# A message-passing layer on one core: messages turned by a scaled W_o1, and a longer prepared start

## The chip, the cores and the metric

The kernel runs on one core of a Trainium2 chip. A core has a matrix engine (TensorE, PE in the profile, its weight loads PEld), VectorE (DVE), ScalarE (ACT), GpSimd (POOL) and SyncE (SP), which only issues DMAs. The engines work beside each other, each through its own instructions in order, and wait for one another by semaphores. The metric is the device time of one execution in microseconds, the median of several runs.

## The reference, cut to what matters

There are 12500 nodes with 128 features and 400000 edges, sorted by `dst`. Each edge carries 20 attributes and a weight.

```python
h   = maximum(layernorm(x), 0) @ W_in2f.T
Wij = smu(edge_attr @ W_f1.T + b_f1) @ W_f2.T + b_f2
Wij = Wij * edge_weight[:, None]
agg = segment_sum(h[dst] * Wij, src, num_segments=12500)
out = x + smu(agg @ W_o1.T + b_o1) @ W_o2.T + b_o2
# smu(z) = ((1 + a) z + (1 - a) z erf(mu (1 - a) z)) / 2,  a = 0.01, mu = 2.5
```

Edges read h at `dst`, which is sorted, and are summed at `src`, which is random. smu is built as a factor times (LIN z + gelu(ZS z)); the factor (GC) is folded into the next weights.

## The kernel before, in words

The edges are cut into 3125 tiles of 128, four tiles make a group (782 groups, the last with one tile), two groups make a superblock, which shares its loads. The 98 blocks of 128 nodes are called bins.

**A group's way.** PE makes the hidden layer of the edge network from the attributes (`hide`, L551, tile pu), ScalarE its gelu (`bend`, L559, ge), VectorE adds the linear part (`smooth`, L567, sm), PE multiplies by W_f2 (`weigh`, L604, pw). For h, VectorE compares each edge's `dst`, relative to a window of rows, with a column of numbers (`pick`, L460, the one-hot tile oh), PE multiplies the window of h by it (`gather`, L585, ph; L583 for the first tiles), ScalarE copies the product (`take`, L593, hg). VectorE multiplies both (`mix`, L614, mt). These messages have the features on the partitions; PE transposes them, a tile at a time (`turn`, L624, pt), and ScalarE writes them, times the edge weight, into a message tile (`send`, L634, ms, six buffers). A message's row has 129 numbers: 128 features and its place in its bin, which VectorE copies from `lo_b` (L631).

**Sorting by src.** VectorE and PE count per bin which slot each edge gets (`bins` L485, `count` L499 to L502, `read` L529, `number` L538, tile ix). GpSimd then writes each tile of 128 messages with one indirect DMA to its slots in a buffer in DRAM (L637, buf). This is 3125 scatters, one queue, in order.

**Pieces.** The superblocks are split into nine pieces (59, 59, 59, 59, 48, 37, 27, 27, 16), each with a slot buffer of its own. While piece k is produced, the slots of piece k-1 are read back (`fetch`, L668, tile rw, four ahead, on SP) and summed: VectorE compares the places with a row of numbers (`choose`, L679, se), PE adds up the messages of a bin in PSUM (`add`, L692, pg), and VectorE adds four bins at a time to `agg` in SBUF (L705). A piece's sums can start only after the last scatter of that piece has landed. Then the next piece goes on; in each group some of these sums (`parts`) stand between its own products. The last piece's sums come after the last scatter, in what is called the tail here. There, for each unit of four bins, PE multiplies agg by W_o1 (`half`, L250), ScalarE makes the gelu (L251), VectorE adds the linear part (`bent`, L255), PE multiplies by W_o2 (L260), VectorE adds x and bias (L264), and SP stores. x is loaded by ScalarE's queue four units ahead and given its bias by GpSimd (`with_bias`, L246).

**The start.** The first 24 tiles (`FEW`, three superblocks) are prepared alone: their `dst` and `src` columns are loaded first, and all of them read h of bin 0. The whole columns come in chunks of 512 tiles (`head_of`): fetched, base of each window read off (`based`, L317), spread over the partitions by PE (`spread`, L326), subtracted, transposed and written to DRAM as rows (`written`), from which each superblock loads its own (`targets`). `binned` and `placed` take bin and place from `src` with a shift and a mask on integers (L360 to L365; L721 to L724 for the first tiles). The rows of h for bins 1 to 3 are made in the `opening`, those of the other 94 bins step by step during piece 0: statistics (L190, L191), normalisation (`normed`, L201), transpose (L207), relu (L210), product (L215), and three bf16 parts of the result.

**Order.** The order on PE, VectorE, ScalarE and SP is the order of the program (`manual_schedule`); GpSimd's is set by a scheduler. In the main loop, `step` is called three times in a group. During the opening a call does two of its 14 steps; afterwards a call does about one of the listed `steps`.

## Time and profile before

| what | value |
|---|---|
| median of 3 runs | 4151.15 us (4150.53 to 4153.11) |
| the profiled execution | 4134.27 us, its span 4132.4 us |
| PE busy | 3500.0 us, 85% |
| DVE busy | 3498.8 us, 85% |
| POOL busy | 3048.9 us, 74% |
| ACT busy | 1854.6 us, 45% |
| granted PE clock, mean | 0.959 |
| DMA | 820.60 MB, mean 199 GB/s |

The profile lists groups of instructions by line, with the number of them, the busy time and the mean of one, and names what ended the idle time before them. A timeline line has the start, the duration, the engine, the line of the kernel, the operation, the tiles (written, then read), the shape or the number of instructions merged, and in brackets the idle time of that engine before it and what ended it. A window line has start and end of the window, its length, the busy time and number of instructions of each engine shown, the granted clock, the busy share of the 16 DMA engines and the GB/s moved.

### The profile page before, as it was taken

To read this page: it belongs to the slowest core of one execution; us is meant where nothing else is said; L and a number is where in the kernel's file an instruction comes from. 1 tells how busy PE (TensorE), PEld (TensorE's weight loads), DVE (VectorE), ACT (ScalarE), POOL (GpSimd) and SP (SyncE) were. 2 spreads that over 40 slices of the span, in tenths; PEclk is the share of its full clock that TensorE was granted. 3 is DMA by queue.
4 is the path that set the end of the run, shared out by engine and by line. 5 is a ranking of instruction groups with operands and counts; after the bars stand their busy time and mean duration, and the time that the engine had idled before them with its cause. 6 is when DMAs were issued, how large, how long until landed. Compare 5 with 4: busy or idle time off the path is not lost. (4 is left out here: it accounts for less than half of the span.)

```text
span 4132.4 us, 67973 instructions
## 1 busy us (share of the span) xinstructions
PE 3500.0 (85%) x18032; PEld 2218.3 (54%) x18032; DVE 3498.8 (85%) x8551; ACT 1854.6 (45%) x4810; POOL 3048.9 (74%) x3173
## 2 busy tenths in 40 slices
PE   6767886988887888869888879998799889898888
PEld 2334444555554555545555546665466556565567
DVE  6898886988887988869888869998799889898887
ACT  3446553544444444435444434444344444444431
POOL 4777777777777777777777777777777777777772
PEclk8999998999998999989999989999899999999999
DMA  4875665766656766647666647776588689787568
GB/s 144 234 198 174 189 186 176 211 193 193 196 156 200 211 197 190 199 140 214 214 189 194 201 149 209 215 212 199 173 233 230 176 244 248 211 234 219 170 184 240
DMA packets 564967, 820.60 MB, mean 199 GB/s; under 512 B 178779, under 2 KB 379234, under 8 KB 564444
## 3 DMA queue, kind: packets, MB, share of 16 engines
q1 hardware_dynamic: 450650, 602.06, 51.1%
q0 software_dynamic: 100320, 207.40, 15.2%
q10 hardware_dynamic: 13602, 6.73, 0.6%
q8 instruction: 143, 2.34, 0.3%
q14 instruction: 252, 2.06, 0.2%
HBM read 442.51 MB, written 373.37 MB: 197 GB/s over the span
## 5 line engine op out<-in xcount | busy, mean ns | idle before, releaser
L637 POOL DMA_INDIRECT buf<-ms,ix x3125 | 3008.6, 963 | 1006.6 <-issue 424.8
L634 ACT ACTIVATE ms<-pt,w_sb 128x128 f32<-128x128 f32 x3125 | 890.9, 368 | 1442.2 <-PE pt L624 848.6
L692 PEld LDWEIGHTS pg<-se,rw 128*128 128x128 f32 x8036 | 1060.6, 193 | 267.0 <-issue 225.1
L692 PE MATMUL pg<-se,rw 128*128 128x128 f32 x8036 | 1154.2, 281 | 8.5 <-DVE se L679 8.5
L485 DVE SCALAR_TENSOR_TENSOR so<-irow_ps,hi_f,so 128x98 f16<-128x98 f32 x3116 | 989.8, 318 | 82.6
L624 PE MATMUL pt<-ident,mt 128*128 128x128 f32 x3125 | 507.2, 286 | 524.7 <-DVE mt L614 522.0
L604 PE MATMUL pw<-sm,w_f 128*128 128x512 f32 x1564 | 902.9, 660 | 42.6 <-DVE sm L567 40.7
L551 PE MATMUL pu<-f,w_f 128*128 128x512 f32 x1564 | 824.5, 610 | 0.0
L559 ACT ACTIVATE ge<-pu 128x512 f32<-128x512 f32 x782 | 469.1, 600 | 555.4 <-PE pu L551 540.2
L679 DVE TENSOR_TENSOR se<-irow_ps,rw 128x1536 f32<-128x1536 f32 (+1 forms) x345 | 587.8, 1704 | 148.4 <-DMA rw<-buf 147.2
L614 DVE SCALAR_TENSOR_TENSOR mt<-pw,b,hg 128x512 f32<-128x512 f32 x782 | 583.3, 746 | 145.8 <-ACT hg L593 133.9
L624 PEld LDWEIGHTS pt<-ident,mt 128*128 128x128 f32 x3125 | 348.2, 143 | 624.5 <-DVE mt L614 618.2
L567 DVE SCALAR_TENSOR_TENSOR sm<-pu,ge 128x512 f32<-128x512 f32 x782 | 534.9, 684 | 151.6 <-ACT ge L559 147.1
L593 ACT ACTIVATE hg<-ph 128x512 f32<-128x512 f32 x782 | 469.1, 600 | 170.0 <-PE ph L585 99.6
L529 DVE TENSOR_REDUCE sl<-pc 128x4 f32<-128x392 f32 x782 | 434.7, 556 | 0.0
L604 PEld LDWEIGHTS pw<-sm,w_f 128*128 128x128 f32 x1564 | 240.3, 194 | 164.2 <-DVE sm L567 136.4
L585 PE MATMUL ph<-oh,hw 126*128 126x512 bf16 x776 | 306.4, 395 | 0.0
L551 PEld LDWEIGHTS pu<-f,w_f 128*128 128x128 f32 x1564 | 258.7, 199 | 59.5 <-issue 52.0
L499 PE MATMUL pc<-so,tri 128*128 128x392 f16 x782 | 260.6, 333 | 1.9 <-DVE so L485 1.1
L501 PE MATMUL pc<-so,rest_h 128*128 128x294 f16 x781 | 227.4, 291 | 0.0
L501 PEld LDWEIGHTS <-rest_h 128*128 128x128 f16 x781 | 77.1, 99 | 272.4 <-issue 272.3
L460 DVE TENSOR_SCALAR oh<-rbc,prow 128x1024 bf16<-128x1024 bf16 x388 | 192.8, 497 | 1.5 <-DMA rbc<-rel_dram 1.5
(151 smaller groups left out, 1357.5 us busy)
## 6 DMA issues: line engine op xcount, KB each, us to landing
rw<-buf SPq DMA_DIRECT2D x292, 774.0 KB
rbc<-rel_dram SPq DMA_DIRECT2D x389, 256.0 KB
buf<-zero SPq DMA_DIRECT2D x243, 387.0 KB
buf<-ms,ix POOLq DMA_INDIRECT x3125
buf<-zero SPq DMA_DIRECT2D x193, 258.0 KB
rw<-buf SPq DMA_DIRECT2D x49, 645.0 KB
f<-in_f_t SPq DMA_DIRECT2D x390, 80.0 KB
hw<-h_dram SPq DMA_DIRECT2D x776, 31.5 KB
```

The lines of the kernel that those rows point to most:

```text
L485: nc.vector.scalar_tensor_tensor(so[:, j], irow_ps[:, :NB], hi_f[:, t + j:t + j + 1], so[:, j - 1] if j else before, op0=ALU.is_equal, op1 ...
L551: nc.tensor.matmul(pu[:, :n], w_f1, loaded[g // PER][0][:, o:o + n], start=True, stop=True)
L559: nc.scalar.activation(ge[:, :n], units_of[g][:, :n], AF.Gelu, scale=ZS)
L567: nc.vector.scalar_tensor_tensor(sm[:, :n], units_of.pop(g)[:, :n], LIN, hidden[g][:, :n], op0=ALU.mult, op1=ALU.add)
L593: nc.scalar.activation(hg[:, :n], rows_of[g][:, :n], AF.Copy)
L604: nc.tensor.matmul(pw[:, :n], w_f2, hidden.pop(g)[:, :n], start=True, stop=True)
L614: nc.vector.scalar_tensor_tensor(mt[:, :n], pws.pop(g)[:, :n], b2, rows_of.pop(g)[:, :n], op0=ALU.add, op1=ALU.mult)
L624: nc.tensor.transpose(pt[:, j, :], mt[:, j * P:(j + 1) * P], ident)
L634: nc.scalar.activation(ms[:, j, 0:P], pt[:, j], AF.Copy, scale=w_sb[:, t + j:t + j + 1])
L637: i = nc.gpsimd.indirect_dma_start(out=bufs[k][:, :], out_offset=bass.IndirectOffsetOnAxis(ap=ix[:, j:j + 1], axis=0), in_=ms[:, j, :], in ...
L679: nc.vector.tensor_tensor(se[:, :m], irow_ps.unsqueeze(1).to_broadcast([P, m, P]), rows_in[c][:, :m, P:P + 1].to_broadcast([P, m, P]), op= ...
L692: nc.tensor.matmul(pgs[0][:, g, :], rows_in[c][:, o, 0:P], sel[c][:, o, :], start=(q == 0), stop=(q == Q[k] - 1))
```

## The change

The transpose of a message tile becomes a product with W_o1, which VectorE scales by LIN once at the start. What is scattered and summed is then already LIN (W_o1 message), so the tail no longer multiplies by W_o1: ScalarE takes the gelu straight from agg, and GpSimd adds the linear part. The tail's second product rotates through four PSUM banks instead of two.

The first 48 tiles (six superblocks) are prepared alone instead of 24, a call of `step` does one opening step instead of two, and each further chunk's columns are fetched one chunk before they are used. W_o1 is loaded at the start by ScalarE's queue.

Bin and place come from fp32 arithmetic: `src` is converted, times 1/128 less almost a half, rounded to a whole number by adding and subtracting 12582912, and the place is `src` less 128 times the bin. The normalisation moves from VectorE to ScalarE (scale and bias per partition; `down` is minus mean over deviation). The place column of a message tile is written by ScalarE instead of VectorE.

```diff
-    nc.vector.tensor_scalar(xn[:, j], x_sb[:, b + j, :], mv[:, b + j, 0:1], rstd[:, b + j:b + j + 1],
-                            op0=ALU.subtract, op1=ALU.mult)
+    nc.scalar.activation(xn[:, j], x_sb[:, b + j, :], AF.Identity, scale=rstd[:, b + j:b + j + 1],
+                         bias=down[:, b + j:b + j + 1])
...
-        FEW = 3 * SUP
+        FEW = 6 * SUP
...
+        def whole_bins(to, sf, si):
+            nc.vector.tensor_copy(sf, si)
+            nc.vector.tensor_scalar(to, sf, 1.0 / P, -(P - 1) / (2.0 * P), op0=ALU.mult, op1=ALU.add)
+            nc.vector.tensor_scalar(to, to, ROUND, None, op0=ALU.add)
+            nc.vector.tensor_scalar(to, to, -ROUND, None, op0=ALU.add)
...
             def binned():
-                nc.vector.tensor_scalar(di[:, z:], si[:, z:], 7, None, op0=ALU.arith_shift_right)
-                nc.vector.tensor_copy(hi_f[:, a + z:a + n], di[:, z:])
+                whole_bins(hi_f[:, a + z:a + n], sf[:, z:], si[:, z:])
             def placed():
-                nc.vector.tensor_scalar(di[:, z:], si[:, z:], P - 1, None, op0=ALU.bitwise_and)
-                nc.vector.tensor_copy(lo_b[:, a + z:a + n], di[:, z:])
+                nc.vector.scalar_tensor_tensor(lo_b[:, a + z:a + n], hi_f[:, a + z:a + n], -float(P), sf[:, z:],
+                                               op0=ALU.mult, op1=ALU.add)
...
+        nc.scalar.dma_start(w_o1, w_o1_t)
         nc.scalar.dma_start(x_sb[:, 1:HEAD, :], bin_rows(x, 1, HEAD - 1))
...
+        nc.vector.tensor_scalar(w_o1, w_o1, LIN, None, op0=ALU.mult)
...
-                nc.tensor.transpose(pt[:, j, :], mt[:, j * P:(j + 1) * P], ident)
+                nc.tensor.matmul(pt[:, j, :], mt[:, j * P:(j + 1) * P], w_o1, start=True, stop=True)
...
-            nc.vector.tensor_copy(ms[:, :n, P], lo_b[:, t:t + n])
+            nc.scalar.activation(ms[:, :n, P], lo_b[:, t:t + n], AF.Copy)
...
+        steps.append(heads_of[0].pop(0))
         for c in range(1, NC):
             if loads:
                 steps.append(loads.pop(0))
-            for f in mine:
+            if c + 1 < NC:
+                steps.append(heads_of[c].pop(0))
+            for f in heads_of[c - 1]:
...
             if opening:
-                for _ in range(2):
-                    if opening:
-                        opening.pop(0)()
+                opening.pop(0)()
                 return
...
         def first_half():
             unit = ready.pop(0)
-            po = ps1.tile([P, GRP * P], F32, name=other(0, ("pu", "ph")))
             ge = edge.tile([P, GRP * P], F32, name="ge")
-            half(unit, po, ge)
-            opened.append((unit, po, ge))
+            nc.scalar.activation(ge[:, :width(unit)], part_of(unit), AF.Gelu, scale=ZS / LIN, bias=bz)
+            opened.append((unit, ge))
         def between():
-            unit, po, ge = opened.pop(0)
+            unit, ge = opened.pop(0)
             sm = edge.tile([P, GRP * P], F32, name="sm")
-            bent(unit, po, ge, sm)
+            nc.gpsimd.tensor_add(sm[:, :width(unit)], part_of(unit), ge[:, :width(unit)])
             smoothed.append((unit, sm))
         def second_half():
             unit, sm = smoothed.pop(0)
-            py = ps1.tile([P, GRP, P], F32, name=other(1, ("pw", "pt")))
+            py = ps1.tile([P, GRP, P], F32, name=other(0, ("pu", "ph", "pw", "pt")))
             rest(unit, sm, py)
```

More of the change, by code (lines that the diff above doesn't have):

```diff
@@ L36 @@
 ZP = 128
+ROUND = 12582912.0
 @with_exitstack
@@ L186, in gnn_kernel @@
     rstd = const.tile([P, NB], F32, name="rstd")
+    down = const.tile([P, NB], F32, name="down")
     def stats(pool, b):
@@ L374, in gnn_kernel @@
         dsf = edge.tile([P, FEW], F32, name="dsf", bufs=1)
+        ssf = edge.tile([P, FEW], F32, name="ssf", bufs=1)
         h_first = const.tile([P, 1, 3, D], BF, name="h_first")
@@ L840, in gnn_kernel @@
         steps = [one["placed"], loads.pop(0), one["limits"]]
+        heads_of = [named(lambda c=c: head_of(c),
+                          ("fetched", "based", "spread", "lowered", "turned", "written", "binned", "placed", "limits"))
+                    for c in range(1, NC)]
+        steps.append(heads_of[0].pop(0))
         for c in range(1, NC):
-            mine = named(lambda c=c: head_of(c),
-                         ("fetched", "based", "spread", "lowered", "turned", "written", "binned", "placed", "limits"))
             if loads:
                 steps.append(loads.pop(0))
-            for f in mine:
+            if c + 1 < NC:
+                steps.append(heads_of[c].pop(0))
+            for f in heads_of[c - 1]:
                 steps.append(f)
@@ L879, in gnn_kernel @@
             i = g - g0
-            if g == 2:
-                assert len(opening) == 2
-                targets(3)
+            if g == (FEW // SUP - 3) * PER:
+                assert not opening
             if g % PER == 0:
@@ L952, in other, with part_of @@
             turns[i] += 1
-            return names[turns[i] % 2]
+            return names[turns[i] % len(names)]
+        def part_of(unit):
+            return agg[:, unit[0] * P:unit[0] * P + width(unit)]
         def first_half():
             unit = ready.pop(0)
-            po = ps1.tile([P, GRP * P], F32, name=other(0, ("pu", "ph")))
             ge = edge.tile([P, GRP * P], F32, name="ge")
-            half(unit, po, ge)
-            opened.append((unit, po, ge))
+            nc.scalar.activation(ge[:, :width(unit)], part_of(unit), AF.Gelu, scale=ZS / LIN, bias=bz)
+            opened.append((unit, ge))
         def between():
-            unit, po, ge = opened.pop(0)
+            unit, ge = opened.pop(0)
             sm = edge.tile([P, GRP * P], F32, name="sm")
-            bent(unit, po, ge, sm)
+            nc.gpsimd.tensor_add(sm[:, :width(unit)], part_of(unit), ge[:, :width(unit)])
             smoothed.append((unit, sm))
```

15 lines of the change are left out of this document (7 added, 8 removed).

## The prediction

> **What bounds the kernel now.** I read the scatter line first (source view of L637), then the timeline of GpSimd, then the scatters counted in windows of 100 us; the chain of waits comes last, since it hands the time from engine to engine and gives POOL 0%.
>
> ```profile
> L637 POOL DMA_INDIRECT buf<-ms,ix x3125: 952/958/1427, 19.1 to 4023.8; - x196
> ...
> 2003.26 0.96 POOL L637 DMA_INDIRECT buf<-ms,ix  x1 [0.30 <-issue]
> 2004.52 0.96 POOL L637 DMA_INDIRECT buf<-ms,ix  x1 [0.30 <-DMA buf<-ms,ix]
> ```
>
> One scatter follows the other every 1.263 us (0.96 busy, 0.30 between, whatever is named as releaser). 3125 x 1.263 = 3947 us, and the first and last start lie 4004.7 us apart. GpSimd's queue is the bound; a group of four scatters is 5.05 us.
>
> ```profile
> 0.00:100.00 100.00, 38.76 (x40) 0.83 0.49 143
> 100.00:200.00 100.00, 74.72 (x78) 0.92 0.82 237
> 200.00:300.00 100.00, 75.92 (x80) 0.93 0.71 197
> ...
> 2000.00:2100.00 100.00, 75.91 (x80) 1.00 0.66 204
> ...
> 3900.00:4000.00 100.00, 69.67 (x73) 1.00 0.71 209
> ```
>
> The full rate is 79 to 80 per window. It is missed at the opening (40), a little to 600 us, and at the end (73). So only four things can move the time: the opening, a producer (PE, VectorE, ScalarE) that falls behind 5.05 us per group, the last piece, and the 108.6 us after the last scatter.
>
> ```profile
> 35.32 0.75 DVE L614 SCALAR_TENSOR_TENSOR mt<-pw,b,hg 128x512 f32<-128x512 f32 x1 [4.96 <-ACT hg L593]
> ...
> 59.20 0.26 DVE L317 COPY base_i<-rw 1x128 int32<-1x128 int32 x1 [7.57 <-DMA rw<-in_dst_col]
> 59.76 2.07 PE L326 MATMUL pg<-base_f,ones 1*128 1x512 f32 x2 [8.15 <-DVE base_f L318]
> ...
> 89.83 0.26 DVE L317 COPY base_i<-rw 1x128 int32<-1x128 int32 x1 [4.46 <-DMA rw<-in_dst_col]
> ```
>
> In the opening VectorE waits for the chunk's columns, with everything queued behind it, and PE then runs at half pace (2.07 us for what took 1.12 at 23.59).
>
> ```profile
> 2006.14 0.90 PE L692 MATMUL pg<-se,rw 128*128 128x128 f32 x6
> 2006.88 0.60 PE L624 MATMUL pt<-ident,mt 128*128 128x128 f32 x4
> 2007.38 1.13 PE L604 MATMUL pw<-sm,w_f 128*128 128x512 f32 x2
> ...
> 4054.51 1.02 PE L250 MATMUL ph<-agg,w_o 128*128 128x512 f32 x2
> 4055.37 1.95 PE L692 MATMUL pg<-se,rw 128*128 128x128 f32 x16
> 4057.19 1.13 PE L260 MATMUL pt<-w_o,sm 128*128 128x128 f32 x8
> 4058.15 1.02 PE L250 MATMUL pu<-agg,w_o 128*128 128x512 f32 x2
> 4059.01 1.95 PE L692 MATMUL pg<-se,rw 128*128 128x128 f32 x16
> ```
>
> A transpose is one PE instruction, a 128x128 f32 product two (x8 for four tiles in L260), each about 0.11 us after the one before (sixteen from 4055.37 to 4057.19). The turn rises from four to eight: +0.44 us of PE per group. In the tail PE is full, 3.64 us per unit.
>
> ```profile
> 4070.00:4080.00 10.00, 10.00 (x77) 8.94 (x76) 8.88 (x11) 2.06 (x3) 4.40 (x4) 1.00 1.02 306
> 4110.00:4120.00 10.00, 10.00 (x76) 8.89 (x75) 6.38 (x10) 2.06 (x3) 3.17 (x3) 1.00 0.53 149
> ```
>
> But until about 4100 us the DMA engines are full there too (share 0.9 to 1.02).
>
> **Opening and first piece.** The first scatter of group 11 starts at 106.85, 87.7 us after the first of all; eleven groups at full rate are 55.6: 32.1 us lost. Of this 7.6 and 4.5 are the two column waits; the fetch one chunk ahead removes them (three steps, or about a group, before use for the first chunk, some twenty for the rest). SP gains no transfer; this one moves ahead of a 12-bin load of x. The rest is latency: six opening steps in a group, and a scatter that waits for the place column, which VectorE writes up to 4 us after the turn (26.23 and 30.13 for group 1). ScalarE now writes it just before the weighting. One opening step per call instead of two, over 48 tiles, leaves per group, on VectorE, about 3.5 us by starts (counting 1.3, mt 0.7, sm 0.6, reading 0.5, small ones 0.4) and one or two steps. Walked through with these rows, turns start near 18, 25, 30, 35, 40, 46 us and then every 5 us, against 17.8, 26.2, 36.1, 42.1, 49.2, 64.3. Costs: eight instead of four turns (+0.44), one more operation on the 48 columns (0.15; the 4.85 us stall of L721 stays, since GpSimd still fills its buffers there), the first normalisation on ScalarE (0.2): the first scatter is 0.8 later. Bounds: -12 (column waits alone) to -32 (all). The walk leaves about 10: **-22**.
> Up to the next piece's first scatter at 655.57 another 8.3 us are lost (548.7 against 107 x 5.05). VectorE, 85 to 90% busy there, sheds 28 us (L201 to ScalarE), 5 us of later column waits and the 0.07 to 0.12 us that each cast holds it; the fp32 binning gives back about 0.7 x 6 = 4 (five operations, 0.43 + 3 x 0.45 + 0.68, for four, 1.79). Bounds 0 to -8: **-5**. ScalarE's additions have no row of their own: the place copy lies between 0.20 (128x1) and 0.37 (128x128), I take 0.2, the nearer in size, in the 0.91 us that ScalarE waits for the turn; a normalisation 0.37 like L634, on an engine 58% busy. The wait for a free ms tile (L631, 37.7 us in 35) moves with the copy to ScalarE, which has the same wait in its own rows (474.5); hg and ge queue behind it, but it lasts only while scatters are waiting. W_o1 now leaves on ScalarE's queue ahead of x for bins 1 to 3, one issue of 0.4 us; those bins are issued at 1.66 and read at 10.78.
>
> **Pieces 1 to 8.** Where the producer isn't held back its groups take 3.04 + 0.111 n when PE is full, n being the L692 instructions in them (4.15 at 10, 4.38 at 12, 4.60 at 14, 4.83 at 16, by starts of L624), and up to 5.8 when se and agg keep VectorE busy and PE waits 0.3 to 1.7 us before the turn. Means, by starts: pieces 1 to 3 4.67 (664.2 to 879.2, 46 groups), then 4.83, 4.81, 5.07, 4.91 and 5.47. Only groups that PE fills, about half, take the 0.44; the others have that wait and lose the cast's 0.1. That gives about 4.85, 5.0, 5.05, 5.25, 5.05, 5.85 (PE alone, 3.48 + 0.111 n: 4.62, 4.89, 5.03, 5.22, 4.77, 5.90). Against 5.05 pieces 1 to 5 and 7 stay hidden under the scatters. After each piece's drain the turn is 6.2 us ahead of its scatter and will need about 1.9, so 4 us are spare: piece 6 loses 0.2 x 51 - 4 = 6, where 2 were lost before; piece 8 0.38 x 27 = 10, less some 3 that the earlier place column saves. Bounds: +4 (VectorE's waits absorb half of piece 8's, too) to +75 (nothing absorbed, worked out below): **+10**, near the low end, since PE's wait before the turn is in the rows.
>
> The Trainium skill ("TensorE: Matmul & The Clock Gate", Terms) says of the transpose mode that it is 4x faster for FP32. By that a turned tile would cost +0.33 us instead of +0.11, and the sum would come out some 670 us higher. L624 and L260 show one to two at equal pace, and the rows decide.
>
> **Tail.** PE loses the half product: 1.82 + 0.96 = 2.78 us per unit instead of 3.64. VectorE keeps 0.68 + 0.68 + 1.75 x 4/6 = 2.5. GpSimd gets a second 1.27 us addition (the shape of L246): 2.55. None binds, but the DMA does: 528 KB of slots, 262 of x and 262 of output per unit, 3.44 us at 306 GB/s. Bounds: -21 (24 x 0.86) to +4, if the additions queue on GpSimd behind with_bias, whose x lands 3.4 to 7.1 us after issue (a loop of three units: 7.1 + 2.55 + 1.0 + 0.7 = 11.4, 3.8 each). I take 3.4 per unit and a little of the idle DMA at the end: **-8**.
>
> **Sum:** -22 - 5 + 10 - 8 = -25. The profiled execution took 4134.27 us (span 4132.4), so 4109. The runs' median is 4151.15, 16.9 above it, without a cause that the page shows; I carry that over: 4126.
>
> **Rivals.** (1) *PE becomes the pace.* If VectorE's waits move along with the turn, every group pays 0.44: pieces 1 to 3 5.11 (3 us each after the spare 4), then 5.27 (16), 5.25 (10), 5.51 (17), 5.35 (11), 5.91 (12), in all +75, net +40: 4191. It decides once the middle costs over 35. For it: PE is 85 to 96% busy. Against: in groups with se mt starts 1.4 to 2.5 us after its hg is ready, so VectorE is what is late. 0.16. (2) *The opening only changes its wait* (hg after its product, a cold PE) and the tail stays at DMA pace: -12 + 0 + 10 - 2 = -4, 4147. For it: the 4.96 us wait, not a DMA's. 0.13. (3) *The tail runs at PE's pace*, the DMA share being partly queueing: -21 there, 4113. For it: no PE or VectorE wait on rw after 4040. 0.17. (4) *A product costs four transposes*: groups 1.32 longer, 0.9 to 1.3 over 5.05 from piece 1 on, about 4780. 0.02. The forecast has 0.52.
>
> **Numbers.** 0.2% is 8 us, about what a measurement can tell from no change: faster is under 4143 (forecast, 3, a little of 2: 0.72), same 0.11, slower 0.17. The range 4104 to 4164 holds the forecast (4110 to 4142 by itself), 3 and 2 and leaves most of 1 out.
>
> **What would show it.** Right: 75 or more scatters in the first 100 us window after the first scatter, no wait on in_dst_col over 2 us, 79 to 80 in windows up to 3300 us, the last scatter near 4007, units of about 3.4 us in the tail with DMA shares near 1. Wrong: windows at 76 or less from 700 us on with GpSimd waiting for ScalarE's ms (rival 1); ScalarE's ms waiting for the turn at 20 to 60 us as before (rival 2); tail units under 3 us (rival 3) or with_bias ahead of the new addition while PE waits (a tail over 108 us).

## The result, and the profile after

The changed kernel takes 4117.11 us (median of 4 runs, 4112.53 to 4125.70); the kernel before, beside it, 4150.84 (4149.83 to 4153.11). The ratio is 0.9919, with a 95% interval of 0.9907 to 0.9930: 34 us faster. The profiled execution took 4118.61 us, its span is 4116.8; for the kernel before these were 4134.27 and 4132.4, so the two profiles show 15.6 of the 34 us.

GpSimd's scatter line (L637, now L648) in the source view of the changed kernel, and its windows, with busy time and count of the scatters, granted clock, DMA share and GB/s:

```profile
L648 POOL DMA_INDIRECT buf<-ms,ix x3125: 952/958/1470, 19.9 to 4010.3; - x196
```

```profile
0.00:100.00 100.00, 55.98 (x58) 0.97 0.65 184
100.00:200.00 100.00, 75.61 (x78) 0.95 0.90 235
...
2000.00:2100.00 100.00, 76.05 (x79) 1.00 0.66 201
3900.00:4000.00 100.00, 68.52 (x72) 1.00 0.66 195
```

The first window holds 58 scatters instead of 40; the middle stands at 79 to 80 as before; the last full window lost one more (72 for 73). The last scatter starts at 4010.3 instead of 4023.8, though the first comes 0.75 us later. In the opening the timeline of the changed kernel reads:

```profile
45.15 1.16 PE L635 MATMUL pt<-w_o,mt 128*128 128x128 f32 x8 [1.64 <-DVE mt L625]
46.35 1.14 ACT L645 ACTIVATE ms<-pt,w_sb 128x128 f32<-128x128 f32 x4 [2.38 <-PE pt L635]
46.52 0.96 POOL L648 DMA_INDIRECT buf<-ms,ix  x1 [0.30 <-issue]
...
58.12 1.30 PE L337 MATMUL pg<-base_f,ones 1*128 1x512 f32 x2 [2.39 <-DVE base_f L329]
...
63.26 0.75 DVE L625 SCALAR_TENSOR_TENSOR mt<-pw,b,hg 128x512 f32<-128x512 f32 x1 [4.79 <-ACT hg L604]
...
66.88 0.96 POOL L648 DMA_INDIRECT buf<-ms,ix  x1 [3.85 <-ACT ms L645]
...
75.63 1.77 PE L635 MATMUL pt<-w_o,mt 128*128 128x128 f32 x8 [2.56 <-DVE mt L625]
...
78.08 0.96 POOL L648 DMA_INDIRECT buf<-ms,ix  x1 [1.14 <-ACT ms L645]
```

ScalarE's message follows the turn by 1.2 us, and between 27.43 and 66.88 GpSimd's scatters follow each other at their ordinary distance (0.30 us idle). The waits on in_dst_col are gone. What is late next is smaller: the base of the next chunk (2.39 us at 58.12), the gathered h (4.79 us at 63.26) and, at 75, a VectorE that is busy with the fp32 bins of that chunk.

For PE this also means another clock. Windows of both kernels with PE's busy time, granted clock, DMA share and GB/s among the engines (PE, PEld, DVE, ACT, POOL), before and after:

```profile
40.00:60.00 20.00, 8.32 (x28) 3.57 (x26) 10.59 (x32) 4.67 (x12) 11.60 (x12) 0.76 0.69 207
60.00:80.00 20.00, 15.27 (x44) 6.94 (x45) 11.91 (x34) 7.08 (x19) 6.32 (x7) 0.73 0.27 69
80.00:100.00 20.00, 13.62 (x39) 6.04 (x38) 13.51 (x41) 6.71 (x18) 13.06 (x14) 0.74 0.94 273
```

```profile
40.00:60.00 20.00, 14.54 (x63) 7.84 (x62) 17.23 (x45) 8.43 (x25) 15.32 (x16) 0.97 0.81 222
60.00:80.00 20.00, 16.28 (x64) 8.58 (x63) 14.09 (x33) 7.67 (x22) 11.96 (x13) 0.86 0.92 270
80.00:100.00 20.00, 17.16 (x76) 9.25 (x74) 18.39 (x53) 11.33 (x32) 15.12 (x17) 1.00 0.78 212
```

The clock is 0.76, 0.73 and 0.74 before, 0.97, 0.86 and 1.00 after: before, PE was also slow in what followed its waits. It still is, for a shorter time. In the changed kernel a window at half clock follows PE's wait of 2.39 us, and a product takes 2.07 us in it that takes 1.02 later:

```profile
58.93:62.34 3.41, 3.41 (x6) 1.22 (x6) 0.00 (x0) 0.00 (x0) 2.50 (x4) 0.50 1.09 305
```

```profile
59.35 2.07 PE L615 MATMUL pw<-sm,w_f 128*128 128x512 f32 x2
...
66.04 1.02 PE L615 MATMUL pw<-sm,w_f 128*128 128x512 f32 x2
```

The gathered h that VectorE awaits until 63.26 stands behind this product, so the largest gap that is left, 3.85 us before the scatter at 66.88, is in part a matter of PE's clock. The Trainium skill ("TensorE: Matmul & The Clock Gate", Part 1) says that PE falls to half its clock when it has been idle for a window of some 3.4 us. The rows agree with the half (2.07 us for the spread after 8.15 us of idling before, where it took 1.12 at 23.59), but here 2.39 us of idling were enough, and so were the 2.56 us before the turn at 75.63, which took 1.77 us instead of 1.16.

In the steady part, the middle of piece 3, and in the tail, PE's timeline reads:

```profile
2000.79 1.06 PE L635 MATMUL pt<-w_o,mt 128*128 128x128 f32 x8
2001.68 1.02 PE L615 MATMUL pw<-sm,w_f 128*128 128x512 f32 x2
...
4057.61 1.16 PE L263 MATMUL pt<-w_o,sm 128*128 128x128 f32 x8 [1.35 <-POOL sm L978]
4058.60 1.95 PE L703 MATMUL pg<-se,rw 128*128 128x128 f32 x16
```

The turn takes 0.89 us by starts (2000.79 to 2001.68); as four transposes it took 0.50. In the tail PE is no longer full; it waits for GpSimd's sum.

To compare many profiles I count the loss of a stretch: the time between the starts of its first scatter and of the next stretch's first, less 5.052 us (4 x 1.263) for each group. The tail is what lies between the last scatter's start and the end of the span. All in us:

| kernel | first scatter | groups 0-10 | groups 11-117 (rest of piece 0) | pieces 1-3 | 4-5 | 6-7 | 8 | tail | span |
|---|---|---|---|---|---|---|---|---|---|
| before | 19.15 | 32.1 | 8.2 | 4.3 | 1.8 | 3.0 | 9.6 | 108.6 | 4132.4 |
| after | 19.90 | 8.0 | 7.5 | 8.3 | 2.7 | 6.3 | 11.9 | 106.5 | 4116.8 |

So by these two: +0.8 for the first scatter, -24.1 in the first eleven groups, -0.7 in the rest of piece 0, +10.5 in pieces 1 to 8, -2.1 in the tail. Two questions are open at this point: which part of the change does what, and where the other 18 us of the timed difference are.

### The profile page after: what moved, and what is told of

The parts are those of the page before. It is cut to its first block, busy times and chain, and to the rows that moved or that the text cites. A ratio compares the mean times of both kernels' runs of the same rounds, so it can differ in the third digit from the quotient of the medians.

```text
span 4116.8 us, 74083 instructions
## 1 busy us (share of the span) xinstructions
PE 3670.0 (89%) x21117; PEld 2553.1 (62%) x21117; DVE 3444.2 (84%) x7657; ACT 1945.8 (47%) x5690; POOL 3084.5 (75%) x3199
## 3 DMA queue, kind: packets, MB, share of 16 engines
q0 software_dynamic: 100320, 207.40, 15.8%
q14 instruction: 253, 2.07, 0.2%
## 4 chain that ended last, share of the span: by engine, by line
PE 39%; DVE 26%; DMA 20%; ACT 6%; issue 5%; POOL 2%; DVEq 0%; SPq 0%; ACTq 0%; POOLq 0%
DMA buf<-ms,ix 18%; PE pt L635 11%; PE pg L703 9%; PE pw L615 8%; DVE se L690 7%; PE pu L562 7%; DVE mt L625 5%; DVE so L496 4%; DVE sm L578 3%; DVE sl L540 3%; ACT ms L645 2%; ACT ge L570 2%; PE ph L596 2%; POOL buf L648 2%; DVE agg L716 1%
## 5 line engine op out<-in xcount | busy, mean ns | idle before, releaser
L648 POOL DMA_INDIRECT buf<-ms,ix x3125 | 3014.1, 965 | 987.6 <-issue 386.8
L635 PE MATMUL pt<-w_o,mt 128*128 128x128 f32 x6250 | 882.3, 285 | 387.2 <-DVE mt L625 384.4
L635 PEld LDWEIGHTS pt<-w_o,mt 128*128 128x128 f32 x6250 | 767.2, 193 | 474.2 <-DVE mt L625 470.5
L615 PE MATMUL pw<-sm,w_f 128*128 128x512 f32 x1564 | 822.8, 608 | 10.3 <-DVE sm L578 8.6
L562 PE MATMUL pu<-f,w_f 128*128 128x512 f32 x1564 | 807.8, 598 | 0.0
L642 ACT ACTIVATE ms<-lo_b 128x4 f32<-128x4 bf16 x782 | 160.0, 205 | 340.8 <-DMA buf<-ms,ix 339.8
L596 PE MATMUL ph<-oh,hw 126*128 126x512 bf16 x770 | 296.9, 386 | 0.0
```

The source lines that it names most:

```text
L562: nc.tensor.matmul(pu[:, :n], w_f1, loaded[g // PER][0][:, o:o + n], start=True, stop=True)
L615: nc.tensor.matmul(pw[:, :n], w_f2, hidden.pop(g)[:, :n], start=True, stop=True)
L635: nc.tensor.matmul(pt[:, j, :], mt[:, j * P:(j + 1) * P], w_o1, start=True, stop=True)
L648: i = nc.gpsimd.indirect_dma_start(out=bufs[k][:, :], out_offset=bass.IndirectOffsetOnAxis(ap=ix[:, j:j + 1], axis=0), in_=ms[:, j, :], in ...
```

## The experiments

Every kernel is told with its median, and with the median of the kernel before run beside it on the same chip. The ledger of all of them stands behind the last one.

### The kernel before, once more

No edit.

> The kernel before, unchanged, to see what its own executions scatter by. The profiled execution of before took 4134.27 us while its timed runs lie at 4149.8 to 4153.1; of the changed kernel the profiled one (4118.61) lies among the timed ones (4112.5 to 4125.7). Theory A: the single profiled execution of before was a fast one by chance, and others span about 4150 with the 16 us in one place: the opening or the last piece, as GpSimd's late starts. Theory B: the 16 us are spread, scatters lasting 5 ns longer each. In the first case windows outside that place show 79 to 80 scatters per 100 us, in the second 78 to 79 everywhere. If the profile is again near 4132, the difference stays open.

Measured: 4146.32 us (10 runs, 4140.97 to 4153.39; ratio 1.0, 0.9990 to 1.0009). The profiled execution took 4141.75 us, 7.5 more than the first profile of the same kernel. Its ledger differs by -0.9, +1.6, +4.9, +1.5, +0.2, +0.2 and, in the tail, +0.1: spread, as in theory B, most of it in pieces 1 to 3 where nothing waits. One profile of this kernel therefore carries several us of chance, and the 16.9 us between profile and median had shrunk to 4.6. By time theory A fits better: the first profiled execution, 4134.27 us, is shorter than all 55 other executions of this kernel on record (4140.97 to 4157.60).

### The turn undone, everything else kept

```diff
-                nc.tensor.matmul(pt[:, j, :], mt[:, j * P:(j + 1) * P], w_o1, start=True, stop=True)
+                nc.tensor.transpose(pt[:, j, :], mt[:, j * P:(j + 1) * P], ident)
...
-            nc.scalar.activation(ge[:, :width(unit)], part_of(unit), AF.Gelu, scale=ZS / LIN, bias=bz)
-            opened.append((unit, ge))
+            half(unit, po, ge)
+            opened.append((unit, po, ge))
```

with the old `between`, the old two banks for the second product, and W_o1 not scaled.

> The changed kernel with messages transposed again and the product with W_o1 back in the tail (PE, with VectorE's linear part); the longer start, the fetch ahead, ScalarE's place column and normalisation and the fp32 bins stay. Theory (scatters bound, terms add): pieces 1 to 8 lose about 19 us to GpSimd idling and long scatters instead of 29, the tail is 108 to 109 us instead of 106.5, groups that PE fills are 0.44 us shorter; span 4116.8 - 10 + 2 = about 4108, and 8 us less than the changed kernel in the timed runs (about 4109). Rival (the turn by W_o1 is worth its place, since the tail is what ends the run): slower than the changed kernel by 5 us or more.

Measured: 4113.58 us (before 4146.83; ratio 0.9921, 0.9904 to 0.9937), span 4107.4. Pieces 1 to 8 lose 17.5 us instead of 29.2, the tail is 111.6 instead of 106.5. The turn's price in the middle and its gain in the tail are both there, and the price is the larger one, as the theory said. But the tail is some 3 us longer than expected, and the time is 3.5 us below the changed kernel's instead of 8.

### The old start in the changed kernel

```diff
-        FEW = 6 * SUP
+        FEW = 3 * SUP
...
-                opening.pop(0)()
+                for _ in range(2):
+                    if opening:
+                        opening.pop(0)()
```

and the further chunks' columns fetched by their own steps again, just before use.

> The changed kernel with the start of before: 24 tiles prepared, two opening steps per call, columns fetched when needed. Theory: the first eleven groups lose about 25 to 30 us again instead of 8 (ScalarE's early place column keeps a few), so 20 us more than the changed kernel: span about 4137, timed about 4137. The column waits of 7.6 and 4.5 us come back. Rival (the gain of the start comes from the place column and the lighter VectorE): the first eleven groups lose under 15 us and the time rises by less than 8.

Measured: 4150.66 us (before 4146.83; ratio 1.0009, 1.0000 to 1.0019). The first eleven groups lose 26.2, as expected, but the time is some 33 us up, not 20: the rest of piece 0 loses 16.8 (7.5 in the changed kernel), with further waits for columns. DVE's timeline of this kernel:

```profile
59.58 0.26 DVE L328 COPY base_i<-rw 1x128 int32<-1x128 int32 x1 [8.36 <-DMA rw<-in_dst_col]
...
123.73 0.26 DVE L328 COPY base_i<-rw 1x128 int32<-1x128 int32 x1 [1.37 <-DMA rw<-in_dst_col]
```

All of the gain of the change hangs on the new start; without it the change brings nothing.

### The tail's sum on VectorE

```diff
-            nc.gpsimd.tensor_add(sm[:, :width(unit)], part_of(unit), ge[:, :width(unit)])
+            nc.vector.tensor_add(sm[:, :width(unit)], part_of(unit), ge[:, :width(unit)])
```

> The changed kernel with the tail's linear part added by VectorE instead of GpSimd, so that no addition stands behind a with_bias that waits for x. VectorE then has 0.68 + 0.68 + 0.68 + 1.17 = 3.2 us per unit. Theory 1 (GpSimd's queue holds the tail: PE waited for it 0.2 to 1.3 us per unit, 2.4 at the end): units from 3.3 to about 3.2 to 3.3, the drain after the last unit 3 us shorter, tail 106.5 to about 103. Theory 2 (DMA paces, shares 0.9 to 1.08): unit pace unchanged at 3.3, and only the drain's 3 us are gained. Rival (VectorE becomes the tail's bound): units at 3.5 or more, tail 108 or more.

Measured: 4118.97 us (before 4146.83; ratio 0.9930, 0.9913 to 0.9947), tail 101.1. PE still waits, now for VectorE:

```profile
4065.61 1.16 PE L263 MATMUL pu<-w_o,sm 128*128 128x128 f32 x8 [0.43 <-DVE sm L978]
```

A unit takes 3.26 us (16 units between the agg additions at 4046.41 and 4098.60) against 3.38 in the changed kernel (15 between 4049.85 and 4100.53). Moving the sum off GpSimd's queue is worth 0.1 us per unit, so GpSimd is not what sets the pace. The tail is shorter by 5.4, but other profiles with the sum on GpSimd gave 101.0 to 106.5 (ledger), so that this shortening proves nothing.

### The changed kernel, once more

No edit.

> The changed kernel once more, beside the three below on one chip. If the 5 us between the kernel with the transpose back (4113.58, on another chip than the changed kernel was timed on) and the changed kernel (4117.11) are real, this one has 4117 to 4119 here again and a tail near 106. The pitch: the profiles so far put 5.04 to 5.06 us on a group that waits for nothing; if the pitch belongs to the chip, the four kernels of this call share it.

Measured: 4115.16 us (4 runs, 4113.24 to 4117.51; before 4149.24; ratio 0.9916, 0.9899 to 0.9932), own time of the profiled execution 4116.91. Its tail is 103.6 where the first profile had 106.5, and its rest of piece 0 loses 5.5 instead of 7.5. The two terms that looked much smaller than forecast in the first profile are partly chance of that execution. The pitch does not go with the chip: the four kernels timed on this one lose 8.1, 5.3, 4.8 and 4.4 us in pieces 1 to 3.

### The 48 tiles and one opening step per call alone

```diff
-        FEW = 3 * SUP
+        FEW = 6 * SUP
...
-                for _ in range(2):
-                    if opening:
-                        opening.pop(0)()
+                opening.pop(0)()
...
```

on the kernel before, with the loads of the superblocks' rows moved to fit.

> The kernel before with only the 48 tiles prepared alone and one opening step per call; bins, place column, fetches, turn and tail as before. Theory (the parts of the opening add up): the first eleven groups lose some 20 instead of 32, since both column waits (7.6 and 4.5 us) stay, so about -12 on the time, 4135. Rival (they only help together, each shows the other's wait next): the first eleven groups still lose 27 or more, and the time falls by under 6.

Measured: 4134.98 us (before 4149.24; ratio 0.9961, 0.9947 to 0.9975), 14 less. The first eleven groups lose 20.3, the theory's 20; but the rest of piece 0 loses 18.1 instead of 8 to 10. The timeline shows why:

```profile
62.35 0.26 DVE L317 COPY base_i<-rw 1x128 int32<-1x128 int32 x1 [8.81 <-DMA rw<-in_dst_col]
...
90.15 0.26 DVE L317 COPY base_i<-rw 1x128 int32<-1x128 int32 x1 [4.98 <-DMA rw<-in_dst_col]
...
95.09 0.95 POOL L637 DMA_INDIRECT buf<-ms,ix  x1 [5.12 <-issue]
...
130.32 0.26 DVE L317 COPY base_i<-rw 1x128 int32<-1x128 int32 x1 [4.17 <-DMA rw<-in_dst_col]
...
134.87 0.95 POOL L637 DMA_INDIRECT buf<-ms,ix  x1 [3.33 <-issue]
```

The second column wait, still at 90 us, ends ahead of group 11, whose first scatter is the one at 95.09. Behind it the third wait, 4.17 us at 130.32, now reaches GpSimd too. With later gaps, some of them without such a wait, those of over half a microsecond cost 11.5 us in groups 11 to 117; in the two profiles of the kernel before they cost 1.9 and 4.4. The span, 4136.3, lies between the two of the kernel before (4132.4 and 4140.0), while the medians differ by 14. The profiled execution is the slowest of this kernel's five, and the first one before was an unusually fast one, so the ledger doesn't show the 14 us, and their agreement with the 12 expected is in part luck.

### The fetch one chunk ahead alone

```diff
-            for f in mine:
+            if c + 1 < NC:
+                steps.append(heads_of[c].pop(0))
+            for f in heads_of[c - 1]:
```

on the kernel before, with the first further chunk's fetch in front of the loop.

> The kernel before with only the further chunks' columns fetched one chunk ahead. Theory (add up): the waits on in_dst_col at 59 and 90 us go, the first eleven groups lose some 20, the time falls by about 12, 4135. Rival (only together): another wait ends at the same place, the first eleven groups lose 27 or more, the time falls by under 6. With few_alone's gain this should come to the 24 us of the opening in the first theory, and to well under that in the rival.

Measured: 4125.25 us (before 4149.24; ratio 0.9944, 0.9927 to 0.9960), 24 less, twice what was expected. In the profile the first eleven groups lose 20.1, 12.0 and 11.1 less than in the two profiles of the kernel before. That is as much as the two waits had been, though one of them is still there, shorter:

```profile
58.59 0.34 DVE L317 COPY base_i<-rw 1x128 int32<-1x128 int32 x1 [3.32 <-DMA rw<-in_dst_col]
```

The other 12 are not in the opening of this profile: its span is 4121.1, 11 to 19 below those of the kernel before.

### The turn by W_o1 and the new tail alone

```diff
-                nc.tensor.transpose(pt[:, j, :], mt[:, j * P:(j + 1) * P], ident)
+                nc.tensor.matmul(pt[:, j, :], mt[:, j * P:(j + 1) * P], w_o1, start=True, stop=True)
...
-            half(unit, po, ge)
-            opened.append((unit, po, ge))
+            nc.scalar.activation(ge[:, :width(unit)], part_of(unit), AF.Gelu, scale=ZS / LIN, bias=bz)
+            opened.append((unit, ge))
```

on the kernel before, with GpSimd's sum, the four banks, and W_o1 loaded early and scaled.

> The kernel before with only the turn by W_o1 and the new tail: LIN folded into W_o1, gelu straight from agg, GpSimd's addition; opening, bins, normalisation and place column as before. Theory: the eight turns cost pieces 1 to 8 about 11 us, as between the changed kernel and the one with the transpose back, the tail gives back 2 to 5; the time rises by 4 to 9, 4151 to 4156. Rival 1 (the place column on ScalarE is what let the turn be cheap: with VectorE's copy still in front of the messages the turn costs more): pieces 1 to 8 lose 35 or more, the time rises by 15 or more. Rival 2 (the turn is free and what differed was the chip): within 2 us of the kernel before less the tail's gain.

Measured: 4156.35 us (10 runs, 4146.85 to 4161.93; before 4149.24; ratio 1.0015, 1.0006 to 1.0025): 7 us slower, the theory's 4 to 9. The part that the change is named for brings nothing by itself. By the ledger pieces 1 to 8 lose 30.7 (18.7 and 25.5 in the two profiles of the kernel before), less than rival 1's 35; the tail is 101.0. What the theory had not named is the rest of piece 0, which loses 17.4 instead of 8 to 10, eleven gaps of over half a microsecond up to group 60. VectorE's timeline shows what lies in front of them:

```profile
127.34 0.26 DVE L317 COPY base_i<-rw 1x128 int32<-1x128 int32 x1 [4.03 <-DMA rw<-in_dst_col]
...
165.34 0.26 DVE L317 COPY base_i<-rw 1x128 int32<-1x128 int32 x1 [4.72 <-DMA rw<-in_dst_col]
```

After 100 us the column waits add up to 13.5 us here, and to 5.2 and 7.7 in the two profiles of the kernel before. Against the means of these two, pieces 1 to 8 lose 8.6 us more, the tail 7.6 less, and the rest of piece 0 8.4 more: by the ledger the 7 us lie there, behind column waits that the fetch ahead takes away. Whether the turn makes them longer, or this execution had long ones, isn't shown.

### Both parts of the new start, nothing else

The two edits above together, on the kernel before.

> The kernel before with both parts of the new start (48 tiles alone, one opening step per call, chunks fetched one chunk ahead) and nothing else of the change. Apart they brought 24 us (fetch) and 14 us (48 tiles). Theory (they add up): first eleven groups lose 8, groups 11 to 118 about 7, time 36 to 38 below the kernel before, 4111 to 4113: below the changed kernel, whose turn costs the rest. Rival 1 (they overlap): 24 to 30 below, 4119 to 4125. Rival 2 (the first scatter's waits are only exchanged): the first eleven groups still lose over 14.

Measured: 4116.04 us (before 4150.37; ratio 0.9917, 0.9903 to 0.9931), 34 less, as much as the whole change. It lies between the theory (36 to 38) and the first rival (24 to 30); first eleven groups 8.0 and the rest 5.8, as the theory had them.

### The turn undone, a second time

The same kernel as above, beside the last one.

> The changed kernel with the transpose, W_o1 and the old tail back, a second time. Against the run beside it that has only the new start, what differs is fp32 bins, the normalisation and the place column on ScalarE. Theory (these bring the first piece some 3 us and pieces 1 to 8 another 3 to 5, by a place column that doesn't wait for VectorE): 4 to 8 below that run. Rival (off the path): within 2 us of it. Against the changed kernel: the alone-turn cost 7 us, so here 5 to 8 below the 4115 to 4117 of the changed kernel, 4108 to 4112; if it is 4114 again, the turn's price in the whole change is under 3 us and the alone-turn's was a matter of the old start.

Measured: 4111.36 us (5 runs, 4106.41 to 4114.08; before 4150.37; ratio 0.9904, 0.9890 to 0.9918): 4.7 below the kernel with only the new start, within the theory's 4 to 8, and 3.8 below the changed kernel on the same chip (3.5 between the first pair), less than the 5 to 8 expected. All of these are below the 8 us that a measurement can tell. The spans of this kernel and of the one with only the new start are the same (4110.6 and 4110.5), so what fp32 bins, normalisation and place column bring together is seen in the times alone; by the ledger pieces 1 to 8 lose 19.0 instead of 22.3, and the tail happens to be 1.5 longer. PE's timeline in the middle and in the tail, for the price of the turn:

```profile
2002.60 0.60 PE L635 MATMUL pt<-ident,mt 128*128 128x128 f32 x4
2003.10 1.12 PE L615 MATMUL pw<-sm,w_f 128*128 128x512 f32 x2
...
4054.37 1.95 PE L703 MATMUL pg<-se,rw 128*128 128x128 f32 x16
...
4058.01 1.95 PE L703 MATMUL pg<-se,rw 128*128 128x128 f32 x16
```

0.50 us for the turn instead of 0.89, and 3.64 per unit in the tail (4054.37 to 4058.01) with PE always busy.

### The place column back on VectorE

```diff
-            nc.scalar.activation(ms[:, :n, P], lo_b[:, t:t + n], AF.Copy)
+            nc.vector.tensor_copy(ms[:, :n, P], lo_b[:, t:t + n])
```

> The changed kernel with the place column written by VectorE again. Theory (from the prediction: each group's VectorE carries 0.07 to 0.2 us more, and the message waits for VectorE's turn in its order, up to 4 us behind the turn): pieces 1 to 8 lose 32 to 40 instead of 28 to 29, groups 11 to 118 lose 10 or more instead of 6 to 8, time up by 5 to 12, 4121 to 4128. Rival 1 (ScalarE pays as much as VectorE saved): within 2 us of the changed kernel. Rival 2 (the copy delays hg and ge on ScalarE): faster by 3 or more.

Measured: 4123.72 us (5 runs, 4120.04 to 4124.30; before 4150.37; ratio 0.9933, 0.9919 to 0.9947), 8.6 above the changed kernel on that chip: the theory's size, but in another place. Pieces 1 to 8 lose 33.7, hardly more than 29.2 and 32.6, and groups 11 to 117 7.9. It is the first eleven groups that lose 13.1 instead of 8.0, as its timeline shows:

```profile
25.60 1.16 PE L635 MATMUL pt<-w_o,mt 128*128 128x128 f32 x8
...
26.80 1.14 ACT L645 ACTIVATE ms<-pt,w_sb 128x128 f32<-128x128 f32 x4 [1.11 <-PE pt L635]
...
28.49 0.16 DVE L642 CAST ms<-lo_b 128x4 f32<-128x4 bf16 x1
...
29.40 0.95 POOL L648 DMA_INDIRECT buf<-ms,ix  x1 [4.62 <-ACT hg L604]
```

(The profile names hg as what ended GpSimd's wait, which the scatter doesn't read.) Group 1 is turned at 25.60 and weighted from 26.80 on, but VectorE comes to its place column only at 28.49, and the scatter starts at 29.40. In the changed kernel the same turn starts at 25.59, and the scatter at 27.43. As long as no messages are in stock, one instruction of 0.16 us behind a busy engine costs its whole delay.

### The tail without x

```diff
-                old_rows(unit, xr, nc.scalar)
-                with_bias(unit, xr, nc.gpsimd)
+                nc.gpsimd.tensor_copy(xr[:unit[2], :unit[1]], bo2[:unit[2]].unsqueeze(1).to_broadcast([unit[2], unit[1], P]))
```

> The changed kernel without the loads of x in the tail; GpSimd copies only the bias, so x is left out of the output. The tail moves 790 KB per unit instead of 1052. Theory (the DMA sets the tail's pace): units of 2.6 to 2.8 us by the adds, where PE's 2.78 takes over, tail 88 to 95 instead of 104 to 106, time down by 10 to 16. Rival 1 (GpSimd's second addition sets it, behind the bias addition): units stay at 3.3, the tail falls by under 4. Rival 2 (the start and the drain of the tail are what is over): units fall to 2.8 and the tail by the same 14, but the drain of 16 us after the last agg addition stays.

x is then missing from the output. Measured: 4099.32 us (before 4150.37; ratio 0.9875, 0.9859 to 0.9891), 15.8 below the changed kernel on that chip; the tail is 86.0. Timeline of PE, and windows (PE, PEld, DVE, ACT, POOL busy, clock, DMA share, GB/s):

```profile
4057.19 1.95 PE L703 MATMUL pg<-se,rw 128*128 128x128 f32 x16
...
4059.87 1.95 PE L703 MATMUL pg<-se,rw 128*128 128x128 f32 x16
```

```profile
4060.00:4070.00 10.00, 10.00 (x92) 10.00 (x91) 8.92 (x11) 2.89 (x4) 6.78 (x9) 1.00 1.04 308
...
4080.00:4090.00 10.00, 10.00 (x92) 10.00 (x91) 6.70 (x9) 2.94 (x5) 6.85 (x7) 1.00 0.35 107
```

and the changed kernel in the same windows:

```profile
4060.00:4070.00 10.00, 8.56 (x74) 8.17 (x74) 7.38 (x8) 2.17 (x3) 6.81 (x7) 1.00 1.02 309
...
4080.00:4090.00 10.00, 8.16 (x68) 7.59 (x68) 6.79 (x8) 2.17 (x3) 7.33 (x7) 1.00 0.99 308
```

A unit takes 2.68 us (4057.19 to 4059.87) and PE is full; with x it takes 3.38 at some 309 GB/s. So x sets the pace of the new tail, and the price is that of its bytes: 1052 KB at 309 GB/s are 3.40 us. But the edit also takes away ScalarE's issue of the load and halves GpSimd's bias instruction (0.61 us instead of 1.27); that the bytes alone do it, and not the wait for a free x tile, is argued and not shown.

### The ledger of all of them

In all rows but the first the profiled execution is one of the timed ones, so the last column says where among them it fell.

| kernel | median us | first scatter | groups 0-10 | 11-117 | pieces 1-3 | 4-5 | 6-7 | 8 | tail | span | median less profiled time |
|---|---|---|---|---|---|---|---|---|---|---|---|
| before | 4151.15 | 19.15 | 32.1 | 8.2 | 4.3 | 1.8 | 3.0 | 9.6 | 108.6 | 4132.4 | 16.9 |
| before, again | 4146.32 | 19.17 | 31.2 | 9.8 | 9.2 | 3.3 | 3.2 | 9.8 | 108.7 | 4140.0 | 4.6 |
| turn alone | 4156.35 | 19.84 | 30.3 | 17.4 | 4.4 | 3.5 | 9.2 | 13.6 | 101.0 | 4144.9 | 9.5 |
| old start in after | 4150.66 | 19.97 | 26.2 | 16.8 | 10.4 | 5.2 | 6.4 | 11.9 | 104.5 | 4146.9 | 2.0 |
| 48 tiles alone | 4134.98 | 19.17 | 20.3 | 18.1 | 5.3 | 3.3 | 4.6 | 9.6 | 110.3 | 4136.3 | -3.1 |
| fetch alone | 4125.25 | 19.16 | 20.1 | 7.0 | 4.8 | 3.0 | 3.4 | 9.4 | 108.8 | 4121.1 | 2.3 |
| new start alone | 4116.04 | 19.17 | 8.0 | 5.8 | 5.5 | 3.4 | 3.6 | 9.8 | 109.8 | 4110.5 | 3.8 |
| turn undone | 4113.58 | 19.27 | 9.0 | 4.4 | 5.4 | 2.6 | 3.0 | 6.5 | 111.6 | 4107.4 | 4.4 |
| turn undone, again | 4111.36 | 19.26 | 9.5 | 6.0 | 5.6 | 3.9 | 3.1 | 6.4 | 111.3 | 4110.6 | -1.0 |
| place column undone | 4123.72 | 19.90 | 13.1 | 7.9 | 7.6 | 3.0 | 8.7 | 14.4 | 102.0 | 4122.3 | -0.5 |
| tail's sum on VectorE | 4118.97 | 19.92 | 8.1 | 7.7 | 11.9 | 4.4 | 5.8 | 12.9 | 101.1 | 4117.5 | -0.3 |
| tail without x | 4099.32 | 19.91 | 7.9 | 7.1 | 9.2 | 3.3 | 8.2 | 13.6 | 86.0 | 4100.7 | -3.1 |
| after | 4117.11 | 19.90 | 8.0 | 7.5 | 8.3 | 2.7 | 6.3 | 11.9 | 106.5 | 4116.8 | -1.5 |
| after, again | 4115.16 | 19.90 | 8.0 | 5.5 | 8.1 | 5.3 | 5.9 | 13.3 | 103.6 | 4115.1 | -1.8 |

The fastest kernel that computes everything is the one with the turn undone, in both of its runs; its distance to the changed kernel, 3.5 and 3.8 us, is below the 8 us that a measurement can tell, but the ledger has its two halves (pieces 1 to 8 12.7 less, the tail 6.4 more, means of two).

## Why the prediction was right, and where its terms were off

The forecast was 4126, in a range of 4104 to 4164; it took 4117. The bound was named rightly: up to the last scatter, every kernel here follows from when GpSimd can scatter.

**Opening, -22.** -24.1 in the first eleven groups and 0.75 for the later first scatter, -23.4 in sum. The walk through the turns (18, 25, 30, 35, 40, 46 us) came out as 18.05, 25.59, 30.06, 34.87, 39.46, 45.15. The fetch ahead was worth 12 us of scatters, the 48 tiles another 12, and both together 24 (against the first profile; about 1 less against the second). That the copy of the place column is part of it was right: 5 us of the first eleven groups come back with it. The sign named beforehand, 75 or more scatters in the 100 us after the first, was too high: 73, since 8.0 us are still lost in these groups, of it 2.4 before the scatter at 27.43, 3.5 before the one at 66.88 and 0.8 before the one at 78.08. The other signs of the opening held: no wait on in_dst_col is left, and from 200 to 3300 us every window holds 79 or 80.

**Rest of piece 0, -5.** Mis-sized in the first pair of profiles (-0.7); over two profiles of each kernel it is 9.0 to 6.5, -2.5. The step that failed is taking all of the 8.3 us lost there for late producers. Gaps of over half a microsecond cost 1.9 and 4.4 us of it in the two profiles before, 2.2 and nothing after. From group 60 to 117 there is no such gap, and 4.0 us are lost in both first profiles: some scatters of these groups last longer than 0.958 us, 20 and 19 of 232 over 1.0. In the kernel with only the new start the same groups lose 4.2 in this way. An earlier message wins none of that back. The long scatters don't fall anywhere; they run beside certain instructions of VectorE. In pieces 1 to 3 of the changed kernel 199 of 1416 scatters overlap with the comparison that makes the one-hot tile (`pick`), and 51 of the 52 long ones are among these; in the first profile before it is 202, and all 39. One such place, by the timeline of the changed kernel:

```profile
2001.16 0.48 DVE L471 TENSOR_SCALAR oh<-rbc,prow 128x1024 bf16<-128x1024 bf16 x1
2001.38 1.09 POOL L648 DMA_INDIRECT buf<-ms,ix  x1 [0.30 <-issue]
```

That `pick` is the cause is not shown, since no run moves it; most scatters beside it (148 of the 199) keep to 1.0 us. The normalisation on ScalarE was also dearer than I took it, 0.50 us for 0.37.

**Pieces 1 to 8, +10.** +10.5 between the first profiles, +8.8 between the means of two. The paces by starts of the turn where nothing holds the group back came out at 4.80, 4.78 and 4.80 for pieces 1 to 3, then 5.00, 4.95, 5.21, 5.03 and 5.65, against 4.85, 5.0, 5.05, 5.25, 5.05 and 5.85. Each term is smaller than forecast where it was placed, 3.0 in pieces 6 and 7 (forecast 4) and 2.9 in piece 8 (forecast 7); the other 2.9 lie in pieces 1 to 5, which I had left at nothing: there the changed kernel has gaps of over half a microsecond worth 1.7 and 3.3 us in its two profiles, the kernel before none and 0.4. They can't be put on the turn: with the transpose back such gaps are worth 1.0 and 2.5 us there, with the new start alone 2.2. Long scatters are more frequent, too: 50 to 55 of 1416 last over 1.0 us in pieces 1 to 3 of the five profiles with both the turn by W_o1 and ScalarE's place column, 34 to 43 in the nine others; why is open. Undoing the turn alone shows its price without the earlier place column: 12.7, of which 6.2 in piece 8.

**Tail, -8.** -2.1 between the first two profiles and -3.6 between the means of two; over all profiles with each tail and the same GpSimd sum, 109.9 (seven) to 103.5 (five), -6.4. The mechanism was right: a unit fell from 3.64 us to 3.38, where 3.4 was forecast, not to PE's 2.78. 24 units of 0.26 us less are 6.2, which is the whole of it; the rest of the 8 I had put on the end of the tail, where the DMA engines idle, and that gain is not there. In the first profile of the changed kernel the end is even longer, since GpSimd waits for the last x, and sums and products follow in turn:

```profile
4100.35 1.26 POOL L249 TENSOR_TENSOR mt<-mt,bo 128x512 f32<-128x512 f32 x1 [2.97 <-DMA mt<-in_x]
4100.53 0.69 DVE L716 TENSOR_TENSOR agg<-agg,pg 128x512 f32<-128x512 f32 x1 [1.04 <-PE pg L703]
4101.57 2.49 POOL L978 TENSOR_TENSOR sm<-agg,ge 128x512 f32<-128x512 f32 x2
...
4102.89 1.35 PE L263 MATMUL pu<-w_o,sm 128*128 128x128 f32 x8 [2.40 <-POOL sm L978]
```

From the last agg addition to the end it takes 16.3 us here and took 12.9 before. In the second profile of the changed kernel it is 12.6, so it isn't there every time.

**The 16.9 us carried over.** This is the step that failed. I took the distance between the first profile and the median for a property of the kernel that would stay. But the profiled execution, at 4134.27 us, was an unusually fast one, 6.7 us below the fastest of the 55 others; whether by chance or by its chip is not on record. The distance was 4.6 in the next profile of the same kernel, 2.0 and 9.5 in two other kernels with the old start, and between -3.1 and 4.4 in all with the 48 tiles or the fetch ahead. So the sum from the profile (-25, against -15.6 by the first pair of spans and -20.2 by the means of two) was too large a gain, the offset was too high, and the two errors partly cancelled: the time fell by 34, 9 more than forecast. That it came so near is in part luck. The fetch ahead shows it by itself: 24 us in the medians, 12 in its profile's opening, 11 to 19 in its span. The median of the kernel before lies 5 and 17 us above its two profiled executions; where the slower executions lose that can't be seen, and stays open. A place that would fit is on record: VectorE's waits on in_dst_col add up to 17.2 and 19.1 us in the two profiles of the kernel before, to 20.0, 20.0 and 26.9 in the three other kernels that fetch just before use, to 3.3 with the fetch ahead alone, and to nothing in the rest.

**Rivals.** PE did not become the pace (pieces 1 to 8 cost 9 to 11, not 35). The opening did not only change its wait: what came next were 8 us. The tail did not reach PE's pace, and did so at once when x was left out. The transpose is half a product, not a quarter: 0.50 us for four, 0.89 for eight instructions. The Trainium skill ("TensorE: Matmul & The Clock Gate", Terms) says of the transpose mode that it is 4x faster for FP32; the rows here show a factor of 1.8.

**What each part is worth, by the times.** New start alone -34; fetch -24, 48 tiles -14; the turn by W_o1 with its tail +7 on the old start, where long column waits came with it, and +4 on the new, which is less than a measurement can tell; place column on ScalarE -9 (against the second run of the changed kernel, on the same chip). The parts don't add up exactly (-24 and -14 make -38, measured -34), within the intervals of the ratios.

## What to carry to other kernels

When one queue is the bound, look for its gaps at the start: a load that is fetched just before use stalled not only its reader but also every engine behind it, and PE's clock, and asking for it one chunk earlier brought 24 us of the 34. An algebraic saving that moves work from a tail of 100 us into a loop of 782 groups costs time in every group that isn't hidden, and its gain in the tail is only what the next limit there (x at 310 GB/s) leaves over. Profile the kernel before at least twice before carrying the distance between a profile and the median into a forecast: the one profiled execution may just have been a fast one.

## What the runs showed of the hardware that was not expected

- The same kernel's profiled span differed by 7.6 us (4132.4 and 4140.0), of which 4.9 lie in 354 groups where no scatter waits. Scatters over 1.0 us account for 1.3 of it (39 and 43 of 1416); the rest is some 3 ns more in each of the others (957.8 and 960.7 ns on average).
- The scatters over 1.0 us in these groups ran beside one VectorE instruction, `pick`, in 39 of 39 and 42 of 43 cases, though only a seventh of all scatters overlap with it.
- PE's clock was halved for 3.4 us after 2.39 and after 2.56 us of idling in the changed kernel's opening (0.50 in 58.93 to 62.34 and in 75.99 to 79.41).
- The timed runs of the kernel before spread from 4143.4 to 4157.6 us on one chip; on another, 19 runs lay between 4144.05 and 4150.85. Executions of one kernel beside each other differed by 3 to 15 us.
- PE at full DMA share: without x the DMA engines showed the same share, 1.04 at 308 GB/s from 4060 to 4070 us, and PE was full all the same. A DMA share near 1 alone does not say that somebody waits for it; that PE's idle time names the wait does.
